# A transformer block's second LayerNorm: which engine centres it and which computes its variance

## The chip, the cores and the metric

The kernel runs on one core of a Trainium2 chip, in fp32 throughout. The metric is the device time of one execution in microseconds, lower is better; a kernel is run several times and the median counts.

## The reference

The input `x` is (16, 128, 96, 96): 16 images, 128 channels, 9216 pixels each. Cut to what matters, the block is:

```python
x_hwc = x.transpose(0, 2, 3, 1)
xn1 = layernorm(x_hwc)                           # over the 128 channels, eps 1e-5
q, k, v = xn1 @ wq.T, xn1 @ wk.T, xn1 @ wv.T     # 8 heads of 16 channels
q, k = l2norm(q), l2norm(k)                      # over the pixels of an image
attn = softmax(q k^T / 4)                        # 16 x 16 for each head, contracted over all pixels
x = x + ((attn @ v) @ wp.T)
xn2 = layernorm(x)                               # over the 128 channels again ("LN2")
h1 = conv1x1(xn2, w_in)                          # 128 -> 512 channels
h2 = depthwise_conv3x3(h1, w_dw)                 # each channel by itself
out = x + conv1x1(gelu(h2), w_out)               # 512 -> 128
```

## The kernel before

**Tiling.** Channels lie on the 128 partitions and pixels along the free dimension. An image has 8 bands of 12 rows (1152 pixels), and a band has 3 units of 4 rows (384 pixels) and 9 tiles of 128 pixels. The 512 hidden channels are 4 chunks of 128. There are 128 bands in all.

**The norms.** Both LayerNorms work on groups of 4 tiles of 128 pixels (`pixels`, 18 groups an image, 288 for all images). TensorE brings a group to pixels on partitions (`forth`), so that channels lie along the free dimension. The variance is found, GpSimd turns it into 1/sqrt(var + eps) with one multiply-add (`variance`) and one power (`power`), ScalarE scales the tile into SBUF (`scaled`), and TensorE transposes it back (`back` in `channels`), after which ScalarE copies it to its place (`place`). In LN1 the scaled tile also goes into a Gram matrix (`gram`, line 678), from which the attention of an image is worked out without q and k ever being formed.

LN1 does not subtract the mean; its weights are centred instead. LN2 has two forms here. In two groups of three, `forth` is a transpose (line 610), VectorE computes mean and variance (`stats`, line 624), `shift` makes -mean/std on VectorE (line 641), and ScalarE applies scale and bias at once (line 668). In every third group (`squares`), `forth` is a product with the matrix I - 1/128 (line 608), which transposes and subtracts the mean together; ScalarE squares each tile and sums the squares in its accumulator (`squared`, line 617), and scales without a bias (line 664). The first groups of image 0 (`early`) use other banks, and VectorE scales half of each.

**The feed-forward part.** A job is one chunk of one band (`conv_job`): TensorE forms the hidden rows (`hidden`, line 896), ScalarE copies them out of PSUM (`kept`, line 901), and the 3x3 depthwise convolution is made of nine shifted products. VectorE does 5 or 6 of them (`tap`, line 914, one pass over 128 x 1152 each), ScalarE does 2 or 3 (`product`, line 909), and DMAs that add into SBUF put the latter together (`add_products`, line 918, issued on GpSimd's queue). GELU follows on ScalarE (line 922).

The last chunk (`PE_CHUNK`) is done otherwise in some bands (`by_matmuls`): TensorE multiplies the normed rows by nine composed 128 x 128 matrices into one PSUM bank, 9 products for each of the 3 units (line 964), and ScalarE applies GELU from PSUM (line 970). Such a band needs no job for that chunk. `by_pe` chooses the bands: every second one, and six of the last eight. Four products with w_out (line 987) and one addition on VectorE (line 994) end a unit, and SyncE's queue stores a band.

An fp32 product is two passes on TensorE in the profile (so 27 products of a convolved band are 54 rows), a transpose is one.

**The order.** Nothing is scheduled at run time. `Plan` collects all operations with an engine, an estimated duration, a place and the buffers they need, plays them through a priority queue, and the order in which they start there is the order in which they are issued. Each engine then works through its own queue strictly in that order and waits at semaphores. `AT` and `STEP` hold the offset of each kind of operation from its band. Buffers that matter: 2 PSUM banks for `forth` (`tr`), 1 for `back`, 4 for the hidden rows, convolutions and outputs together (`h`), 10 SBUF buffers for the results of the convolution (`h3`) and 5 for ScalarE's products (`pr`).

Of the kernel before, what the change touches and what calls it, by code (L numbers as in the profile page):

```python
# [9 lines left out]
F32 = mybir.dt.float32  # L10
AF = mybir.ActivationFunctionType
# [6 lines left out]
UR = 4  # L18
BR = 12
PE_CHUNK = 3  # L20
PE_BANDS = (0,)
PE_OF = 2
PE_LAST = (0, 1, 2, 4, 5, 7)
TINY = 1e-20
UNIT_MIN = 1e-18
# [3 lines left out]
QT, QB = 4, 1  # L29
H_BANKS = 4  # L30
X1_BUFS, XB_BUFS, PR_BUFS, H3_BUFS, ZT_BUFS = 2, 6, 5, 10, 3
SQ_OF, SQUARED = 3, (0,)
IN_TURN = ("tr", "h3", "pr", "xb", "x1")
AT = dict(
    weights=165.45, zeros=121.05, load_a=-89.25, forth_a=1.7, stats_a=-26.4, variance_a=10.25, power_a=75.3,
    scaled_a=-4.95, gram=3.45, back_a=-204.3, place_a=63.85, attention=-94.6, mix=-102.65, residual=301.65,
    mixed=-85.2, add_x=89.65, forth_b=3.2, stats_b=-63.7, variance_b=165, power_b=182.8, shift_b=-95.45,
    scaled_b=139.5, back_b=-179.7, place_b=-67.95, squared=39.9, halo=146.15, hidden=5.1, kept=-94.75,
    products=-76.65, add_last=123.75, tap=7.3, add_first=-186.6, gelu=51.85, conv=4.7, conv_gelu=7, out=8.4,
    add=-77.85, store=98.15,  # L40
)
STEP = dict(scaled=0.3, hidden=0.1, products=0.5, tap=0.166, conv=1.6, conv_tap=0.03, out=0.8, out_part=0.05)
SLACK = 300
# [164 lines left out]
def tile_restormer_block(  # L208
# [142 lines left out]
    def at(kind, place):  # L351
        return place + AT[kind]
# [34 lines left out]
    def act(ns, p, f, r, w):  # L387
        op("ACT", ns, p, f, r, w, ns + 150 + SLACK, ns + 150)
# [158 lines left out]
    def norm(i, second, place_of):  # L547
# [5 lines left out]
        def xtok(u):  # L553
            return (x_key(i, u // UPB, second), (i, u // UPB), u % UPB)
# [34 lines left out]
        def pixels(s, m):  # L589

            d = {}
            qs = range(m * QB, (m + 1) * QB)
            early = i == 0 and (not second or m < EARLY)
            key_ = "h" if early else "tr"
            by_dve = QT // 2 if early else 0
            squares = second and not early and m % SQ_OF in SQUARED

            def forth(q):
                if early:
                    d["pT", q] = bank((name, q)).rearrange("p (t c) -> p t c", c=P)  # L600
                else:
                    d["pT", q] = p_tr.tile([P, QT, P], F32, tag="tr", name=f"pT_{name}_{q}")
                for k in range(QT):
                    b, j = divmod(q * QT + k, TPB)
                    xt = (xbs if x_key(i, b, second) == "xb" else x1s)[i, b]
                    xk = xt[:, j * P : (j + 1) * P]
                    if squares:
                        nc.tensor.matmul(d["pT", q][:, k, :], lhsT=xk, rhs=centring, start=True, stop=True)  # L608
                    else:
                        nc.tensor.transpose(d["pT", q][:, k, :], xk, ident)  # L610

            def squared(q):
                if q == qs[0]:
                    d["st"] = small.tile([P, QB * QT], F32, tag="ss", name=f"ss_{name}_{m}")
                for k in range(QT):
                    t = (q - qs[0]) * QT + k
                    nc.scalar.activation(junk, d["pT", q][:, k, :], AF.Square, accum_out=d["st"][:, t : t + 1])

            def stats(j):

                if j == 0:
                    d["st"] = small.tile([P, QB * QT // 2, 6], F32, tag="st", name=f"st_{name}_{m}")
                h, k = divmod(2 * j, QT)
                nc.vector.bn_stats(  # L624
                    d["st"][:, j, :], d["pT", qs[h]][:, k : k + 2, :].rearrange("p t c -> p c t")
                )

            def variance():
                if not squares:
                    d["mv"] = d["st"].rearrange("p j (t v) -> p (j t) v", v=3)  # L630
                of = d["st"] if squares else d["mv"][:, :, 2]
                ve = d["ve"] = small.tile([P, QB * QT], F32, tag="ve", name=f"ve_{name}_{m}")
                nc.gpsimd.tensor_scalar(ve, of, 1.0 / C, EPS, ALU.mult, ALU.add)  # L633

            def power():
                rstd = d["rstd"] = small.tile([P, QB * QT], F32, tag="rstd", name=f"rstd_{name}_{m}")
                nc.gpsimd.tensor_tensor(rstd, d["ve"], mhalf, ALU.pow)  # L637

            def shift():
                nb = d["nb"] = small.tile([P, QB * QT], F32, tag="nb", name=f"nb_{name}_{m}")  # L640
                nc.vector.scalar_tensor_tensor(nb, d["mv"][:, :, 1], -1.0, d["rstd"], ALU.mult, ALU.mult)  # L641

            def zT(q):
                zTs[q] = zT_bufs[plan.slot["zT", (name, q)]]
                return zTs[q]

            def also_scaled(q):
                for k in range(by_dve):
                    t = (q - qs[0]) * QT + k
                    if not second:  # L650
                        nc.vector.tensor_scalar(
                            zT(q)[:, k, :P], d["pT", q][:, k, :], d["rstd"][:, t : t + 1], None, ALU.mult
                        )
                        continue
                    nc.vector.tensor_scalar(
                        zT(q)[:, k, :P], d["pT", q][:, k, :], d["mv"][:, t, 1:2], d["rstd"][:, t : t + 1],
                        ALU.subtract, ALU.mult,
                    )

            def scaled(q):  # L660
                for k in range(by_dve, QT):
                    t = (q - qs[0]) * QT + k
                    if not second or squares:
                        nc.scalar.activation(  # L664
                            zT(q)[:, k, :P], d["pT", q][:, k, :], AF.Copy, scale=d["rstd"][:, t : t + 1]
                        )
                        continue
                    nc.scalar.activation(  # L668
                        zT(q)[:, k, :P], d["pT", q][:, k, :], AF.Identity,
                        bias=d["nb"][:, t : t + 1], scale=d["rstd"][:, t : t + 1],  # L670
                    )

            def gram(q):
                if q == 0:
                    grams[i] = p_g.tile([P, 4 * P], F32, tag="g", name=f"g_{i}")
                for k in range(QT):
                    zt = zTs[q][:, k, :]
                    nc.tensor.matmul(  # L678
                        grams[i][:, : P + 1], lhsT=zt[:, :P], rhs=zt,
                        start=(q == 0 and k == 0), stop=(q == NU * TPU // QT - 1 and k == QT - 1),  # L680
                    )

            trs, bt = [(key_, (name, q)) for q in qs], ("batch", (name, m))
            for q, tr in zip(qs, trs):
                units = {t // TPU: None for t in range(q * QT, (q + 1) * QT)}
                pe((220 if squares else 110) * QT, at("forth" + ab, s), lambda q=q: forth(q), [xtok(u) for u in units], [tr])
            for q, tr in zip(qs, trs) if squares else ():
                act(QT * 295, at("squared", s), lambda q=q: squared(q), [tr], [bt])
            for j in range(0 if squares else QB * QT // 2):
                dve(341, at("stats" + ab, s), lambda j=j: stats(j), [trs[2 * j // QT]], [bt])  # L690
            op("POOL", T_VARIANCE, at("variance" + ab, s), variance, [], [bt], T_VARIANCE + 33 + SLACK)
            op("POOL", T_POWER, at("power" + ab, s), power, [], [bt], T_POWER + 33 + SLACK)
            if second and not squares:
                dve(80, at("shift" + ab, s), shift, [], [bt])
            for h, (q, tr) in enumerate(zip(qs, trs)):
                zt, sh = ("zT", (name, q)), s + STEP["scaled"] * h
                if by_dve:
                    dve(by_dve * 240, at("scaled" + ab, sh), lambda q=q: also_scaled(q), [tr, bt], [(*zt, 0)])
                act((QT - by_dve) * (343 if second and not squares else 250), at("scaled" + ab, sh), lambda q=q: scaled(q), [tr, bt], [(*zt, 1)])
                if not second:  # L700
                    pe(QT * 220, at("gram", sh), lambda q=q: gram(q), [(*zt, 0), (*zt, 1), ("w", "ones")], [("g", i)])

# [369 lines left out]
```

## Time and profile before

| | |
|---|---|
| median of 3 runs | 4224.22 us (4222.87 to 4229.13) |
| the profiled execution: its own time | 4229.13 us |
| its span in the trace | 4227.4 us |
| granted TensorE clock, mean | 0.998 |
| busy in the span: TensorE matmuls, weight loads | 4190.0 us, 2725.4 us |
| busy: VectorE, ScalarE, GpSimd | 4036.8, 3780.7, 2473.4 us |
| DMA, q0 (the adding DMAs), share of 16 engines | 83.6% |
| DMA, q1 (loads and stores), share of 16 engines | 9.9% |

The profile is of one execution. Busy time is the union of the instructions' spans on an engine. Instructions of ScalarE, VectorE and TensorE overlap their successors by some 0.1 to 0.2 us, so the mean duration of one instruction is longer than what one more of its kind costs. In the timeline the cost is read as the distance from one start to the next where no wait is noted. A row of the timeline gives start, duration, engine, line, operation, result and operands, the count of merged instructions, and in brackets the idle time before it with its releaser.

### The profile page before, as it was taken

Reading aid. Unit: us, or ns where it says so; the run is one execution under the profiler, and the core shown is the slowest. Engines: PE = TensorE matmul, PEld = TensorE weight load, DVE = VectorE, ACT = ScalarE, POOL = GpSimd, SP = SyncE. Lnnn points to the kernel's source line nnn. Section 1 sums busy time; section 2 is a strip of 40 time slices with the busy share of each in tenths; the row PEclk is TensorE's granted clock in tenths of the full one; section 3 lists DMA queues with packets and bytes.
Section 4 is the critical chain, followed back from the end, with each engine's and each line's share of the span. In section 5 each row is a group of like instructions: output and inputs, shape, how many; then the busy total and the mean of one; then the engine's idle time right before and its main releaser. Section 6 shows DMA issues by size and latency. Waiting matters only on the chain. (4 is left out here: it accounts for less than half of the span.)

```text
span 4227.4 us, 53445 instructions
## 1 busy us (share of the span) xinstructions
PE 4190.0 (99%) x17833; PEld 2725.4 (64%) x17833; DVE 4036.8 (95%) x4394; ACT 3780.7 (89%) x7722; POOL 2473.4 (59%) x2373
## 2 busy tenths in 40 slices
PE   8999999999999999999999999999999999999999
PEld 6666666666666666666666666666666666666555
DVE  6999999999999999999999999999999999999998
ACT  4999999999999999999999999999989989998885
POOL 3657567565665746656475565656656566565442
PEclk9999999999999999999999999999999999999999
DMA  2999999999999999999999999999989999998997
GB/s 85 190 198 205 204 201 209 199 206 192 212 197 201 204 193 206 197 200 209 189 204 200 204 201 193 210 198 205 202 182 205 201 199 197 200 206 179 198 191 157
DMA packets 203940, 827.71 MB, mean 196 GB/s; under 512 B 23568, under 2 KB 24976, under 8 KB 203664
## 3 DMA queue, kind: packets, MB, share of 16 engines
q0 software_dynamic: 164160, 672.47, 83.6%
q1 hardware_dynamic: 37152, 151.01, 9.9%
q8 instruction: 141, 2.31, 0.2%
q10 hardware_dynamic: 2352, 0.81, 0.1%
q14 instruction: 135, 1.11, 0.1%
HBM read 148.26 MB, written 75.50 MB: 53 GB/s over the span
## 5 line engine op out<-in xcount | busy, mean ns | idle before, releaser
L914 DVE SCALAR_TENSOR_TENSOR h<-h,ratio,h 128x1152 f32<-128x1152 f32 x2104 | 2924.9, 1407 | 14.8
L909 ACT ACTIVATE pr<-h,ratio 128x1152 f32<-128x1152 f32 x1018 | 1291.1, 1286 | 41.2 <-DMA h<-pr 18.8
L964 PE MATMUL h<-xn,comp 128*128 128x384 f32 x3564 | 1250.1, 485 | 0.2 <-ACT h L901 0.2
L987 PE MATMUL h<-h,woutT 128*128 128x384 f32 x3072 | 1133.6, 488 | 2.2 <-ACT h L901 2.2
L896 PE MATMUL h<-xn,winT 128*128 128x384 f32 (+1 forms) x2676 | 1054.9, 500 | 2.4 <-ACT h L901 1.7
L964 PEld LDWEIGHTS h<-xn,comp 128*128 128x128 f32 x3564 | 648.6, 189 | 394.3 <-issue 5.6
L918 POOL DMA_DIRECT2D pr<-pr x573 | 542.2, 961 | 582.6 <-ACT pr L909 388.9
L901 ACT COPY h<-h 128x384 f32<-128x384 f32 (+1 forms) x1338 | 659.9, 516 | 159.8 <-PE h L896 152.1
L987 PEld LDWEIGHTS h<-h,woutT 128*128 128x128 f32 x3072 | 557.2, 190 | 335.4 <-issue 19.5
L914 DVE SCALAR_TENSOR_TENSOR h<-h,ratio 128x1152 f32<-128x1152 f32 x446 | 627.4, 1409 | 66.2 <-ACT h L901 54.7
L896 PEld LDWEIGHTS h<-xn,winT 128*128 128x128 f32 x2676 | 476.8, 190 | 282.0 <-issue 47.9
L918 POOL DMA_DIRECT2D h<-pr x445 | 429.3, 966 | 383.6 <-DVE h L914 94.0
L922 ACT ACTIVATE h<-h 128x1152 f32<-128x1152 f32 x448 | 531.5, 1187 | 24.7 <-DMA h<-pr 21.5
L637 POOL TENSOR_TENSOR rstd_b<-ve_b,mhalf 128x4 f32<-128x4 f32 x288 | 502.1, 1744 | 14.4
L637 POOL TENSOR_TENSOR rstd_a<-ve_a,mhalf 128x4 f32<-128x4 f32 x288 | 497.2, 1727 | 12.7 <-POOL ve_a L633 0.2
L633 POOL TENSOR_SCALAR ve_a<-st_a 128x4 f32<-128x4 f32 x288 | 296.0, 1028 | 287.7 <-DVE st_a L624 282.7
L664 ACT ACTIVATE zT<-pT_a,rstd_a 128x128 f32<-128x128 f32 x1080 | 315.1, 404 | 16.1 <-POOL rstd_a L637 15.9
L678 PEld LDWEIGHTS g<-zT 128*128 128x128 f32 x2304 | 294.1, 192 | 41.0 <-issue 2.6
L633 POOL TENSOR_SCALAR ve_b<-st_b 128x4 f32<-128x4 f32 x194 | 217.6, 1122 | 172.4 <-DVE st_b L624 165.8
L678 PE MATMUL g<-zT 128*128 128x129 f32 x2304 | 306.9, 276 | 0.0
L668 ACT ACTIVATE zT<-pT_b,nb_b,rstd_b 128x128 f32<-128x128 f32 x756 | 287.0, 477 | 12.1 <-DVE nb_b L641 11.8
L563 PE MATMUL h<-xn,mwT 128*128 128x384 f32 x768 | 282.0, 488 | 1.9 <-ACT zT L668 0.6
(178 smaller groups left out, 3950.5 us busy)
## 6 DMA issues: line engine op xcount, KB each, us to landing
pr<-pr POOLq DMA_DIRECT2D x573, 576.0 KB, 7.3
h<-pr POOLq DMA_DIRECT2D x445, 576.0 KB, 7.4
x<-in_x_dram SPq DMA_DIRECT2D x128, 576.0 KB, 6.8
out_dram<-x SPq DMA_DIRECT2D x127, 576.0 KB, 6.7
x<-in_x_dram POOLq DMA_DIRECT2D x122, 576.0 KB, 7.3
out_dram<-x SPq DMA_DIRECT2D x3, 192.0 KB, 1.9
weights<-in_L_conv_w_in_dram ACTq DMA_DIRECT2D x1, 256.0 KB, 11.1
weights<-in_L_conv_w_out_dram ACTq DMA_DIRECT2D x1, 256.0 KB, 12.0
```

Source lines behind the costliest of these rows:

```text
L633: nc.gpsimd.tensor_scalar(ve, of, 1.0 / C, EPS, ALU.mult, ALU.add)
L637: nc.gpsimd.tensor_tensor(rstd, d["ve"], mhalf, ALU.pow)
L664: nc.scalar.activation(zT(q)[:, k, :P], d["pT", q][:, k, :], AF.Copy, scale=d["rstd"][:, t : t + 1])
L678: nc.tensor.matmul(grams[i][:, : P + 1], lhsT=zt[:, :P], rhs=zt, start=(q == 0 and k == 0), stop=(q == NU * TPU // QT - 1 and k == QT - 1),)
L896: nc.tensor.matmul(rows(ph), lhsT=winT[:, n, :], rhs=window(xn, r0 + r, e - r, 1), start=True, stop=True)
L901: nc.scalar.copy(window(h1_, r, e - r, 1), rows(d.pop(("ph", r))))
L909: nc.scalar.activation(to, shifted(t), AF.Copy, scale=ratio[:, n, t : t + 1])
L914: nc.vector.scalar_tensor_tensor(h3, shifted(t), ratio[:, n, t : t + 1], onto, ALU.mult, ALU.add)
L918: nc.gpsimd.dma_start(out=to, in_=d["pr", t], accum_op=ALU.add)
L922: nc.scalar.activation(h3, h3, AF.Gelu)
L964: nc.tensor.matmul(d["pc"], lhsT=comp[:, t, :], rhs=window(xn, r0 + dy, UR, dx), start=(t == 0), stop=(t == 8),)
L987: nc.tensor.matmul(rows(d["po"]), lhsT=woutT[:, n, :], rhs=h3s[g, n][:, s * UR : (s + 1) * UR, :], start=(k == 0), stop=(k == NCH - 1),)
```

## The change

All LN2 groups, those of the start included, now take the form with the centring product and ScalarE's squares; the form with transpose, VectorE statistics, `shift` and bias is gone. The chunk that TensorE convolves is taken in 3 bands of 7 in place of 1 of 2, and in the same six of the last eight. All offsets in `AT` are new, and so the order of all queues. The core of the diff:

```diff
-PE_BANDS = (0,)
-PE_OF = 2
+PE_BANDS = (0, 2, 4)
+PE_OF = 7
...
-SQ_OF, SQUARED = 3, (0,)
+ACT_STATS = (False, True)
...
-    weights=165.45, zeros=121.05, load_a=-89.25, forth_a=1.7, stats_a=-26.4, variance_a=10.25, power_a=75.3,
...
+    weights=280.5, zeros=97.3, load_a=-104.05, forth_a=0.1, stats_a=-61.75, variance_a=134.45, power_a=-94.85,
...
-            squares = second and not early and m % SQ_OF in SQUARED
+            squares = ACT_STATS[second]
...
-                    if squares:
-                        nc.tensor.matmul(d["pT", q][:, k, :], lhsT=xk, rhs=centring, start=True, stop=True)
+                    if second or squares:
+                        nc.tensor.matmul(
+                            d["pT", q][:, k, :], lhsT=xt[:, j * P : (j + 1) * P], rhs=centring, start=True, stop=True
+                        )
                     else:
-                        nc.tensor.transpose(d["pT", q][:, k, :], xk, ident)
+                        nc.tensor.transpose(d["pT", q][:, k, :], xt[:, j * P : (j + 1) * P], ident)
...
-            def shift():
-                nb = d["nb"] = small.tile([P, QB * QT], F32, tag="nb", name=f"nb_{name}_{m}")
-                nc.vector.scalar_tensor_tensor(nb, d["mv"][:, :, 1], -1.0, d["rstd"], ALU.mult, ALU.mult)
...
                 for k in range(by_dve, QT):
                     t = (q - qs[0]) * QT + k
-                    if not second or squares:
-                        nc.scalar.activation(
-                            zT(q)[:, k, :P], d["pT", q][:, k, :], AF.Copy, scale=d["rstd"][:, t : t + 1]
-                        )
-                        continue
                     nc.scalar.activation(
-                        zT(q)[:, k, :P], d["pT", q][:, k, :], AF.Identity,
-                        bias=d["nb"][:, t : t + 1], scale=d["rstd"][:, t : t + 1],
+                        zT(q)[:, k, :P], d["pT", q][:, k, :], AF.Copy, scale=d["rstd"][:, t : t + 1]
                     )
...
-            if second and not squares:
-                dve(80, at("shift" + ab, s), shift, [], [bt])
```

By the built programs the change is, in instructions: squares on ScalarE 376 to 1152 tiles; LN2 products with the centring matrix 376 to 1152 and LN2 transposes 776 to none; VectorE statistics of LN2 388 to none and `shift` 194 to none; convolved bands 66 to 57, so products of line 964 from 1782 to 1539; jobs of that chunk 62 to 71; taps on VectorE 2550 to 2604; ScalarE's products 1018 to 1036 and with them the adding DMAs.

More of the change, by code (lines that the diff above doesn't have):

```diff
@@ L31 @@
 X1_BUFS, XB_BUFS, PR_BUFS, H3_BUFS, ZT_BUFS = 2, 6, 5, 10, 3
-SQ_OF, SQUARED = 3, (0,)
+ACT_STATS = (False, True)
 IN_TURN = ("tr", "h3", "pr", "xb", "x1")
 AT = dict(
-    weights=165.45, zeros=121.05, load_a=-89.25, forth_a=1.7, stats_a=-26.4, variance_a=10.25, power_a=75.3,
[L36 to L40, printed above, removed]
+    weights=280.5, zeros=97.3, load_a=-104.05, forth_a=0.1, stats_a=-61.75, variance_a=134.45, power_a=-94.85,
+    scaled_a=-25.95, gram=-72.35, back_a=-145.1, place_a=40.1, attention=-101.25, mix=-124.65, residual=-29.95,
+    mixed=-182.6, add_x=36.1, forth_b=0.15, stats_b=-184.75, variance_b=-169.9, power_b=-123, scaled_b=234.65,
+    back_b=-57.35, place_b=165.45, halo=235.55, hidden=3.95, kept=-96.65, products=47.7, add_last=-139.2,
+    tap=0.3, add_first=64.75, gelu=172.5, conv=4.1, conv_gelu=-0.05, out=8.2, add=-30.9, store=115.05,
 )
@@ L605, in forth @@
                     xt = (xbs if x_key(i, b, second) == "xb" else x1s)[i, b]
-                    xk = xt[:, j * P : (j + 1) * P]
-                    if squares:
-                        nc.tensor.matmul(d["pT", q][:, k, :], lhsT=xk, rhs=centring, start=True, stop=True)
+                    if second or squares:
+                        nc.tensor.matmul(
+                            d["pT", q][:, k, :], lhsT=xt[:, j * P : (j + 1) * P], rhs=centring, start=True, stop=True
+                        )
                     else:
-                        nc.tensor.transpose(d["pT", q][:, k, :], xk, ident)
+                        nc.tensor.transpose(d["pT", q][:, k, :], xt[:, j * P : (j + 1) * P], ident)
             def squared(q):
@@ L628, in variance @@
             def variance():
-                if not squares:
-                    d["mv"] = d["st"].rearrange("p j (t v) -> p (j t) v", v=3)
-                of = d["st"] if squares else d["mv"][:, :, 2]
+                of = d["st"] if squares else d["st"].rearrange("p j (t v) -> p (j t) v", v=3)[:, :, 2]
                 ve = d["ve"] = small.tile([P, QB * QT], F32, tag="ve", name=f"ve_{name}_{m}")
@@ L649, in also_scaled @@
                     t = (q - qs[0]) * QT + k
-                    if not second:
-                        nc.vector.tensor_scalar(
-                            zT(q)[:, k, :P], d["pT", q][:, k, :], d["rstd"][:, t : t + 1], None, ALU.mult
-                        )
-                        continue
                     nc.vector.tensor_scalar(
-                        zT(q)[:, k, :P], d["pT", q][:, k, :], d["mv"][:, t, 1:2], d["rstd"][:, t : t + 1],
-                        ALU.subtract, ALU.mult,
+                        zT(q)[:, k, :P], d["pT", q][:, k, :], d["rstd"][:, t : t + 1], None, ALU.mult
                     )
@@ L662, in scaled @@
                     t = (q - qs[0]) * QT + k
-                    if not second or squares:
-                        nc.scalar.activation(
-                            zT(q)[:, k, :P], d["pT", q][:, k, :], AF.Copy, scale=d["rstd"][:, t : t + 1]
-                        )
-                        continue
                     nc.scalar.activation(
-                        zT(q)[:, k, :P], d["pT", q][:, k, :], AF.Identity,
-                        bias=d["nb"][:, t : t + 1], scale=d["rstd"][:, t : t + 1],
+                        zT(q)[:, k, :P], d["pT", q][:, k, :], AF.Copy, scale=d["rstd"][:, t : t + 1]
                     )
@@ L685, in pixels @@
                 units = {t // TPU: None for t in range(q * QT, (q + 1) * QT)}
-                pe((220 if squares else 110) * QT, at("forth" + ab, s), lambda q=q: forth(q), [xtok(u) for u in units], [tr])
+                pe((220 if second or squares else 110) * QT, at("forth" + ab, s), lambda q=q: forth(q), [xtok(u) for u in units], [tr])
             for q, tr in zip(qs, trs) if squares else ():
-                act(QT * 295, at("squared", s), lambda q=q: squared(q), [tr], [bt])
+                act(QT * 295, at("stats" + ab, s), lambda q=q: squared(q), [tr], [bt])
             for j in range(0 if squares else QB * QT // 2):
@@ L698, in pixels @@
                     dve(by_dve * 240, at("scaled" + ab, sh), lambda q=q: also_scaled(q), [tr, bt], [(*zt, 0)])
-                act((QT - by_dve) * (343 if second and not squares else 250), at("scaled" + ab, sh), lambda q=q: scaled(q), [tr, bt], [(*zt, 1)])
+                act((QT - by_dve) * 250, at("scaled" + ab, sh), lambda q=q: scaled(q), [tr, bt], [(*zt, 1)])
                 if not second:
```

## The prediction

> **What bounds the kernel now.** I read the busy shares first, then the starts in TensorE's timeline, then the chain and the waits.
>
> ```profile
> PE 4190.0 (99%) x17833; PEld 2725.4 (64%) x17833; DVE 4036.8 (95%) x4394; ACT 3780.7 (89%) x7722; POOL 2473.4 (59%) x2373
> q0 software_dynamic: 164160, 672.47, 83.6%
> ```
>
> Three engines and the DMAs look nearly full, so busy shares alone decide nothing. TensorE's starts do:
>
> ```profile
> 2008.98 1.05 PE L608 MATMUL pT_b<-centring,x 128*128 128x128 f32 x8
> 2009.86 0.81 PE L964 MATMUL h<-xn,comp 128*128 128x384 f32 x2
> ...
> 2017.88 0.49 PE L711 MATMUL pB_a<-ident,zT 128*128 128x128 f32 x3
> 2018.21 0.60 PE L610 MATMUL pT_a<-ident,x 128*128 128x128 f32 x4
> 2018.65 0.81 PE L964 MATMUL h<-xn,comp 128*128 128x384 f32 x2
> 2019.29 1.05 PE L678 MATMUL g<-zT 128*128 128x129 f32 x8
> ...
> 4208.37 15.49 PE h L987 x48
> ```
>
> The first rows are the timeline, the last is the chain's end, where the kernel finishes on 48 passes at 0.323 us. No row has idle time in brackets: each starts when the one before has streamed. Four transposes take 2018.65 - 2018.21 = 0.44 us, 0.109 each; eight centring passes take 0.88 us, 0.111 each; a pass over 384 columns takes 0.322. The lower quartile of the distances between starts, over the whole trace, gives the same paces, 0.402 for 480 columns and 0.109 for 129. So TensorE's work in passes is: line 964, 3564 x 0.322 = 1148 us; line 987, 3072 x 0.322 = 989; line 896, 2236 x 0.323 + 440 x 0.402 = 899; line 563, 768 x 0.322 = 247; Gram and back transposes, 4608 x 0.109 = 502; forward transposes, 1928 x 0.109 = 210; centring, 752 x 0.111 = 83; attention and weights about 57. Together 4135 us of a span of 4227.4. The other 92 are 6 before the first pass, 4 after the last, and 82 of waits and jitter, 27 of them in the first 200 us. From then on TensorE loses 55 us in 4000. It is the bound, and the clock can't move much: the granted mean is 0.998.
>
> **The other engines**, by the same paces: VectorE 3972 us (2550 taps at 1.325, 964 statistics at 0.341, 384 additions at 0.467, small ones), ScalarE 3653. ScalarE's rows:
>
> ```profile
> 2006.08 1.19 ACT L664 ACTIVATE zT<-pT_a,rstd_a 128x128 f32<-128x128 f32 x4
> 2007.09 3.62 ACT L909 ACTIVATE pr<-h,ratio 128x1152 f32<-128x1152 f32 x3
> 2010.53 0.65 ACT L715 ACTIVATE xn<-pB_b,b 128x384 f32<-128x384 f32 x1
> ...
> 2054.24 0.28 ACT L617 ACTIVATE junk<-pT_b 128x128 f32<-128x128 f32 x1
> 2054.41 0.20 ACT L617 ACTIVATION_READ_ACCUMULATOR junk<-pT_b 128x1 f32 x1
> 2054.63 1.28 ACT L922 ACT_TABLE_LOAD   x1
> 2055.92 1.16 ACT L922 ACTIVATE h<-h 128x1152 f32<-128x1152 f32 x1
> 2056.99 1.49 ACT L668 ACTIVATE zT<-pT_b,nb_b,rstd_b 128x128 f32<-128x128 f32 x4
> 2058.36 0.27 ACT L860 COPY y<-g 128x128 f32<-128x128 f32 x1
> ```
>
> A square with its accumulator read costs 2054.63 - 2054.24 = 0.39 us (0.394 over the trace), a scaling with bias (2058.36 - 2056.99)/4 = 0.342, without it 1.01/4 = 0.252 (0.249 over the trace), one of the big products 3.44/3 = 1.147, a GELU of a band 1.054.
>
> **The change on TensorE**, which is on the path all along. Nine bands lose 54 passes each: 9 x 54 x 0.322 = -156.5 us. Their jobs add two products of 480 and one of 384 columns: 9 x (4 x 0.402 + 2 x 0.322) = +20.3. 776 tiles turn from a transpose into two centring passes: 776 x (0.222 - 0.109) = +87.7. The sum is -48.5: TensorE's work falls to 4087 us.
>
> *A rule against it.* The row says that a centring product costs 0.222 us where a transpose costs 0.109. The Trainium skill (Perfetto Trace Analysis, section Transposes) says that a logical transpose should be issued as a transpose and not as an ordinary product. By the rule alone the change loses the 87.7 us; the trace agrees on the price, but not on the verdict, since convolutions worth more leave the same engine.
>
> *A rule on the bound.* Between starts nothing waits, in rows with 0.19 us of weight load under 0.32 us of matmul. The same page (section Identifying the Most-Contended Engine) would have TensorE judged by weight-load busy time, not matmul busy time. By it (64%) there is a third of the engine free, ScalarE at over 95% would bind after the change, and the 48.5 us would be worth nothing: about 4224 us. I go by the starts.
>
> **On VectorE:** 9 jobs of 6 taps, 54 x 1.325 = +71.6; 388 statistics x 0.341 = -132.3; 194 shifts x 0.073 = -14.2; ten half-scalings lose their subtraction, -0.7. Together -75.6: 3897 us, all under TensorE's cover.
>
> **On ScalarE:** 776 squares x 0.394 = +305.7; 766 scalings x (0.342 - 0.249) = -71.2; in nine bands three copies (2 x 0.439 + 0.359), two products (2 x 1.147) and one GELU of a band for three of a unit (1.054 - 3 x 0.370), 9 x 3.48 = +31.3. Together +266: 3919 us. That lies beside TensorE's 4087 with 168 us to spare, much as VectorE's 3972 lay beside 4135 with 163. Without that cover it is the first rival.
>
> **On GpSimd and the DMAs:** its variance and power counts stay. 18 more adding DMAs cost 18 x 0.96 = 17 us of issue on an engine at 59%. One holds the 16 DMA engines 0.836 x 4227/1140 = 3.10 us (1140 with the 122 that add x), so q0 rises by 56 to 3590 us, 85.7% of the new span. ScalarE's own waits on DMAs are 59 us now (21.5 + 18.8 + 18.6); scaled by the idle share of q0, 16.4% to 14.3%, they become 68, which ScalarE's spare time hides. Loads and stores keep their number on SyncE's queue.
>
> **The wait that moves.** In 194 groups GpSimd's variance now waits for ScalarE's squares instead of VectorE's statistics. Behind it in GpSimd's queue stand adding DMAs, and for those wait GELU and then line 987. The rows for the two forms are these:
>
> ```profile
> POOL ve_b L633 <- DVE st_b L624: 165.8, 90, 6.4
> POOL ve_b L633 <- ACT junk L617: 129.6, 65, 7.0
> ACT h L901 <- PE h L896: 152.1, 266, 3.4
> DVE h L914 <- ACT h L901: 54.7, 42, 3.6
> PE pB_b L711 <- ACT zT L664: 1.9, 2, 1.6
> ```
>
> Per group that is 0.85 us now (165.8/194) against 1.38 (129.6/94): 288 groups would make GpSimd wait about 397 us where it waits 295, and it has over 1700 us without busy time. TensorE itself lost next to nothing to such chains (last row).
>
> **What the new order costs** the trace can't show. TensorE was fed beside one engine with 163 us to spare; it will be fed beside two with 168 and 190. Its gaps of over 0.2 us after the start sum to 26 us. From below, half of these could go (-13); from above stand the rivals' prices. I take +13, half of the 26 again for the second tight engine, as the nearest row is VectorE's: tight, and nearly harmless. Span: 4087 + 92 + 13 = 4192. The profiled span lies 3.2 us above the median of the runs (4227.4 against 4224.2), so I say 4189. What is late next would be ScalarE.
>
> **Rival 1, ScalarE becomes the bound (slower).** Its queue is strict, and today it idles 574 us beside its 3653. Part of that is being early, part is bursts that a fuller queue doesn't remove: waits on TensorE (lines 901, 970, 717, 715, 572: 152.1 + 38.3 + 41.8 + 36.5 + 10.6 = 279), on DMAs 59, on GpSimd and VectorE about 40, together 378. If all stay, the span is 3919 + 378 = 4297, 4294 by the median. It decides from 317 us of remaining waits on (4236 - 3919, 0.2% over the median before). For it: the largest of these waits, line 901, comes 266 times and isn't one of slack only. Against it: VectorE ran with 255 us between pace and span, and ScalarE would have 273 at my forecast.
>
> **Rival 2, lumpier bands.** Every seven bands now hold two in a row without TensorE's convolution. Such a band asks VectorE for 23 taps x 1.325 + 3.5 = 34.0 us (3.5: the rest of its 3897, over 128 bands) and TensorE for (4087 - 57 x 17.4 - 71 x 2.25)/128 + 2.25 = 25.2. Before, no two such bands came together. If none of the second one's difference is bridged, TensorE waits 8.8 us in 17 places: 150 us, 4339. With half of it bridged it is 75 us in place of my 13, 4251. It costs the whole gain at 48 us. Ten `h3` buffers, two and a half bands, speak against it.
>
> **How the numbers follow.** My forecast has 0.55, with its own range 4163 (gaps halve) to 4215; rival 1 has 0.22, from 4233 to 4294; rival 2 has 0.18, from 4205 to 4339; a start or an end that the new order makes worse has 0.05, around 4220. The range 4163 to 4262 leaves out a little below (0.03), half of rival 1 and a quarter of rival 2, some 0.18 in all. A measurement of this kernel can tell 0.2%, 8.4 us, from no change. Faster: 0.53 of the forecast and 0.03 of rival 2, 0.56. Within 0.2%: 0.10, from the last case and rival 2. Slower: rival 1 and most of rival 2, 0.34.
>
> **What would show it.** Right: TensorE's starts still close up, with paces 0.322 and 0.111 and no bracketed idle time; distances beyond the pace near 95 us in all; ScalarE at about 95 to 97% busy, VectorE near 94%. Rival 1 shows as waits of TensorE's and VectorE's rows on ScalarE (zT, h of line 901's successor) of a hundred us and more; rival 2 as waits that return every seven bands, some 230 us apart. If the accumulator read costs more in a full queue than 0.394 us a square, ScalarE's term is wrong; if TensorE's paces stretch, all of it is.

## The result and the profile after

The changed kernel takes 4255.39 us (median of 4 runs, 4252.32 to 4258.21) against 4225.37 of the kernel before: ratio 1.0070, 95% interval 1.0053 to 1.0088. It is slower by 30 us; 36 less were forecast. The page of its profiled execution (span 4256.5 us), the lines that answer to those of before:

```profile
PE 4178.0 (98%) x18177; PEld 2737.5 (64%) x18177; DVE 3971.5 (93%) x3866; ACT 3952.2 (93%) x9301; POOL 2434.6 (57%) x2391
...
q0 software_dynamic: 166752, 683.09, 82.8%
```

By the same paces as in the prediction, TensorE's work is now 4087 us, ScalarE's 3919 and VectorE's 3912 (forecast 4087, 3919 and 3897). The counting was right; what lies around TensorE's work was not. I call that the *waits* of a kernel from here on: its median less the sum of TensorE's paces, good to some 3 us. Before they were 90, after they are 168.

The waits of the weight loads show the same. Each row gives what waited, for whom, the sum in us, the count and the longest; after, and then before:

```profile
PEld h L876 <- ACT h L881: 26.1, 44, 1.6
...
PEld pB_b L691 <- ACT zT L651: 19.0, 56, 3.0
```

```profile
PEld h L896 <- ACT h L901: 7.6, 18, 1.3
...
PEld pB_b L711 <- ACT zT L664: 5.1, 10, 2.2
```

All such waits on ScalarE together grew from 81 to 212. So far this reads as rival 1. But the waits come in a rhythm. The next rows are the changed kernel's windows, cut at the last output product (line 967) of each band of one period of seven: start and end, length, busy us and count of each engine, granted clock, DMA share and GB/s. The bands, in order: not convolved on TensorE, convolved, not, convolved, not, **not**, convolved.

```profile
2590.30:2617.30 27.00, 26.96 (x101) 16.38 (x100) 25.28 (x21) 26.48 (x62) 11.02 (x12) 1.00 0.84 175
2617.30:2647.50 30.20, 30.20 (x112) 18.68 (x111) 29.92 (x27) 25.73 (x58) 14.80 (x16) 1.00 1.01 209
2647.50:2679.10 31.60, 31.60 (x146) 21.30 (x145) 28.93 (x28) 30.94 (x73) 20.02 (x19) 1.00 1.00 210
2679.10:2697.70 18.60, 18.60 (x74) 11.51 (x73) 18.60 (x19) 18.18 (x40) 11.28 (x12) 1.00 1.00 223
2697.70:2738.70 41.00, 40.94 (x190) 27.52 (x189) 41.00 (x39) 39.87 (x100) 28.62 (x26) 1.00 0.98 205
2738.70:2783.00 44.30, 38.44 (x173) 26.91 (x172) 39.26 (x38) 38.30 (x88) 33.06 (x25) 0.92 0.85 179
2783.00:2824.00 41.00, 39.80 (x192) 27.34 (x191) 33.88 (x35) 36.67 (x90) 24.95 (x25) 1.00 0.95 195
```

The steady bands leave TensorE no hole; the second of the double bands has 44.30 - 38.44 = 5.9 us without a matmul, the one after it 1.2. Summed over bands 4 to 119, the distances of TensorE's starts beyond the pace are 29.3 us in the stretches that end with the first band of a double, 39.9 in those of the second, and 7.9 to 11.8 in each of the other five. That is rival 2's mark.

One such hole, in the timeline of the changed kernel, by start:

```profile
2745.61 0.41 DVE L624 BATCH_NORM_STATS2 st_a<-pT_a 128x6 f32<-128x256 f32 x1
...
2747.27 1.40 DVE L894 SCALAR_TENSOR_TENSOR h<-h,ratio 128x1152 f32<-128x1152 f32 x1
2747.74 10.30 POOL L631 TENSOR_SCALAR ve_a<-st_a 128x4 f32<-128x4 f32 x1
2748.60 5.39 DVE L894 SCALAR_TENSOR_TENSOR h<-h,ratio,h 128x1152 f32<-128x1152 f32 x4
2753.92 1.40 DVE L894 SCALAR_TENSOR_TENSOR h<-h,ratio 128x1152 f32<-128x1152 f32 x1
2755.25 2.73 DVE L894 SCALAR_TENSOR_TENSOR h<-h,ratio,h 128x1152 f32<-128x1152 f32 x2
...
2758.12 1.03 POOL L635 TENSOR_TENSOR rstd_a<-ve_a,mhalf 128x4 f32<-128x4 f32 x1
2759.19 1.14 ACT L651 ACTIVATE zT<-pT_a,rstd_a 128x128 f32<-128x128 f32 x4 [4.64 <-POOL rstd_a L635]
2759.61 2.09 PE L660 MATMUL g<-zT 128*128 128x129 f32 x8 [2.94 <-ACT zT L651]
```

The last statistics before it end at 2746.02. GpSimd's multiply-add on 128 x 4 elements, which takes 0.18 us at its shortest, starts at 2747.74 and ends at 2758.04, when VectorE's eight taps in a row end. Then power, scaling and TensorE follow at once. ScalarE, named as TensorE's releaser, had itself been waiting. This was in no rival; it is theory F below, where it is also counted how much of the 168 us comes this way.

### The profile page after: what moved, and what is told of

It is laid out like the page before. It is cut to its first block, busy times and chain, and to the rows that moved or that the text cites. A ratio compares the mean times of both kernels' runs of the same rounds, so it can differ in the third digit from the quotient of the medians.

```text
span 4256.5 us, 55284 instructions
## 1 busy us (share of the span) xinstructions
PE 4178.0 (98%) x18177; PEld 2737.5 (64%) x18177; DVE 3971.5 (93%) x3866; ACT 3952.2 (93%) x9301; POOL 2434.6 (57%) x2391
## 3 DMA queue, kind: packets, MB, share of 16 engines
q0 software_dynamic: 166752, 683.09, 82.8%
## 4 chain that ended last, share of the span: by engine, by line
PE 37%; ACT 11%; DVE 4%; DMA 2%; issue 2%; POOL 1%; POOLq 0%; ACTq 0%; DVEq 0%
PE h L967 9%; PE h L944 9%; PE h L876 8%; DVE h L894 4%; ACT pr L889 3%; PE pT_b L606 2%; PE h L562 2%; PE g L660 2%; ACT zT L651 2%; ACT h L902 1%; ACT h L881 1%; ACT junk L617 1%; DMA h<-pr 1%; PE pB_b L691 1%; PE pB_a L691 1%
## 5 line engine op out<-in xcount | busy, mean ns | idle before, releaser
L894 DVE SCALAR_TENSOR_TENSOR h<-h,ratio,h 128x1152 f32<-128x1152 f32 x2149 | 2971.2, 1409 | 17.4
L889 ACT ACTIVATE pr<-h,ratio 128x1152 f32<-128x1152 f32 x1036 | 1344.9, 1305 | 33.9 <-DMA h<-pr 19.3
L944 PE MATMUL h<-xn,comp 128*128 128x384 f32 x3078 | 1109.8, 486 | 0.8 <-ACT h L881 0.7
L944 PEld LDWEIGHTS h<-xn,comp 128*128 128x128 f32 x3078 | 560.4, 189 | 344.2 <-ACT h L881 5.3
L898 POOL DMA_DIRECT2D h<-pr x454 | 471.6, 1039 | 237.8 <-DVE h L894 45.9
L902 ACT ACTIVATE h<-h 128x1152 f32<-128x1152 f32 (+1 forms) x457 | 549.7, 1206 | 10.3 <-DMA h<-pr 10.0
L635 POOL TENSOR_TENSOR rstd_b<-ve_b,mhalf 128x4 f32<-128x4 f32 x288 | 481.0, 1670 | 13.6
L631 POOL TENSOR_SCALAR ve_b<-ss_b 128x4 f32<-128x4 f32 x288 | 224.3, 779 | 441.6 <-ACT junk L617 441.3
L617 ACT ACTIVATE junk<-pT_b 128x128 f32<-128x128 f32 x1132 | 330.1, 292 | 89.2 <-PE pT_b L606 60.7
L651 ACT ACTIVATE zT<-pT_b,rstd_b 128x128 f32<-128x128 f32 x1132 | 335.3, 420 | 11.7 <-POOL rstd_b L635 11.5
L651 ACT ACTIVATE zT<-pT_a,rstd_a 128x128 f32<-128x128 f32 x1080 | 319.0, 417 | 14.8 <-POOL rstd_a L635 14.5
```

The lines of the kernel that those rows point to most:

```text
L651: nc.scalar.activation(zT(q)[:, k, :P], d["pT", q][:, k, :], AF.Copy, scale=d["rstd"][:, t : t + 1])
L889: nc.scalar.activation(to, shifted(t), AF.Copy, scale=ratio[:, n, t : t + 1])
L894: nc.vector.scalar_tensor_tensor(h3, shifted(t), ratio[:, n, t : t + 1], onto, ALU.mult, ALU.add)
L898: nc.gpsimd.dma_start(out=to, in_=d["pr", t], accum_op=ALU.add)
L902: nc.scalar.activation(h3, h3, AF.Gelu)
L944: nc.tensor.matmul(d["pc"], lhsT=comp[:, t, :], rhs=window(xn, r0 + dy, UR, dx), start=(t == 0), stop=(t == 8),)
```

## The experiments

The theories as they stood: A, ScalarE is too full (rival 1); B, double bands (rival 2); C, the order was planned with squares at 295 ns where they cost 394; D, both ScalarE and VectorE hold a part; E, neither. F came last: unbroken runs of taps keep GpSimd out, and TensorE waits for 1/sqrt. Where a kernel leaves instructions out, the queues keep their order, so that only the load changes.

**One square in four left out.** TensorE's work 4086, waits 149.

```diff
-                for k in range(QT):
+                for k in range(QT - 1):
```

> The changed kernel in the same order of every queue, but ScalarE leaves out the square of the fourth tile of each LN2 group (a constant stands in for its sum): 288 squares less, 288 x 0.394 = 113 us of ScalarE's 3919, and nothing else. TensorE's work stays at 4087 us; the changed kernel lost 169 us around it (span 4256). Theory A, ScalarE is too full and TensorE waits for it: most of the 77 us of added waits go, about 4185 to 4205. Theory B, the two bands in a row without convolution are the cause and VectorE is late there: little changes, 4240 to 4255. Theory C, the order was planned with squares that are too cheap (295 ns in the plan, 394 in the trace; three squares cost 1.18 us, what the plan has for four): 4185 to 4205 as well, told apart from A by the run with the corrected plan.

4235.24 us (4229.09 to 4244.13), ratio 1.0028 (1.0019 to 1.0037). 20 us came back, between the forecasts of A and B: neither alone.

**71 taps left out, in the bands that aren't convolved.**

```diff
+            if n == PE_CHUNK and t == left[-1] and not last:
+                return
```

> The changed kernel in the same order, but VectorE leaves out the last tap of each job of the last chunk: 71 taps less, 71 x 1.325 = 94 us, all of them in bands that TensorE doesn't convolve. Theory B (lumps, VectorE late in the double bands): VectorE's 34.0 us for such a band become 32.7, and a good part of the added waits goes, 4200 to 4225. Theory A or C: little changes, 4240 to 4255.

4244.06 us, ratio 1.0046 (1.0031 to 1.0061): 11 us.

**The same number of taps left out evenly.**

```diff
+            if n == 0 and g % 9 in (0, 2, 4, 6, 8) and t == left[-1]:
+                return
```

> The changed kernel in the same order, but VectorE leaves out the last tap of the first chunk's job in 71 bands spread evenly: the same 94 us off VectorE, not aimed at the bands without convolution. Theory B: it helps less than taking them out where the lump is, 4220 to 4240. A VectorE that is merely too full everywhere would show the same gain in both. Theory A or C: 4240 to 4255.

4242.73 us, ratio 1.0041 (1.0027 to 1.0055): 13 us, no less than where the lump is. Relief aimed at the lump bought no more than relief elsewhere.

**The plan's price corrected.**

```diff
-                act(QT * 295, at("stats" + ab, s), lambda q=q: squared(q), [tr], [bt])
+                act(QT * 394, at("stats" + ab, s), lambda q=q: squared(q), [tr], [bt])
```

> The changed kernel with one number of the plan changed: a square is planned at 394 ns, as the trace has it, in place of 295. No work is added or left out; the order of the queues moves. Theory C: the waits fall to those of the kernel before, 4190 to 4215. Theory A or B: within 20 us of the changed kernel, 4235 to 4275.

4281.84 us, ratio 1.0136 (1.0121 to 1.0151): worse than any theory had it. The offsets in `AT` fit one set of prices; with another they are just other offsets. So where a later kernel is said to have its offsets searched anew, it has the corrected price and offsets from a new random search with the plan as its measure, equally long for each.

**The same with offsets searched anew.** Same work as the changed kernel.

> The changed kernel's work to the last instruction, with a square planned at 394 ns as measured, and with all offsets searched anew for that plan (in the run with the corrected price alone the old offsets no longer fitted: 4282). Theory C (an order planned with a wrong price): 4190 to 4220. Theories A, B, D: the loads are the same, so the waits stay, 4240 to 4265.

4248.51 us, ratio 1.0048 (1.0033 to 1.0063), waits 164. Price and search together are worth 7 us. C falls.

**Three of four squares left out; 199 taps left out; both.**

```diff
-                for k in range(QT):
+                for k in range(1):
...
+            if n in (0, PE_CHUNK) and t == left[-1] and not last:
+                return
```

> The changed kernel in the same order of every queue, ScalarE leaves out three of the four squares of each LN2 group (a constant stands in for their sums): 864 x 0.394 = 340 us off ScalarE, whose 3919 us become 3579, less than the 3653 of the kernel before. TensorE's 4087 stay. Leaving out one square in four gave 20 us. Theory A (a full ScalarE is what TensorE waits for): TensorE's waits fall to those of the kernel before, about 4180 to 4195. Theory B (two bands in a row without convolution, VectorE late there): a floor of about 4220 to 4235 is left. Theory D (both engines hold a part): 4200 to 4220.

> The changed kernel in the same order, VectorE leaves out the last tap of every job of the first and the last chunk: 199 taps, 199 x 1.325 = 264 us off VectorE's 3912. Leaving out 71 gave 11 to 13 us. Theory B: 4190 to 4215. Theory A: nothing beyond the 13 us had already, 4235 to 4245. Theory D: 4215 to 4235.

> The changed kernel in the same order with both left out, 340 us of squares on ScalarE and 264 us of taps on VectorE, so that TensorE's 4087 us stand over 3579 and 3648. Theories A, B and D: TensorE has nothing to wait for but the start, 4165 to 4190. If it stays over 4200, the waits come from neither engine's load but from the order itself or the DMAs (theory E).

The busy lines of the three, in that order:

```profile
PE 4155.6 (98%) x18177; PEld 2747.0 (65%) x18177; DVE 3968.8 (94%) x3866; ACT 3694.0 (87%) x7573; POOL 2499.7 (59%) x2395
```

```profile
PE 4170.1 (98%) x18177; PEld 2734.4 (64%) x18177; DVE 3725.2 (88%) x3667; ACT 3955.7 (93%) x9301; POOL 2337.4 (55%) x2391
```

```profile
PE 4142.5 (99%) x18177; PEld 2742.9 (66%) x18177; DVE 3723.2 (89%) x3667; ACT 3696.0 (88%) x7573; POOL 2398.6 (57%) x2395
```

4227.65 us, ratio 1.0002 (0.9992 to 1.0012); 4240.98, 1.0031 (1.0019 to 1.0044); 4187.29, 0.9904 (0.9889 to 0.9919). The first lies in B's range, the second in A's, the third in that of A, B and D. Alone they give 28 and 14 us, together 68, and waits of 104. With ScalarE at 87%, looser than the 89% of before, some 143 us of waits are still there: A falls as the whole cause. A part of why the two give more together is in the traces: with the squares out ScalarE's waits for 1/sqrt from GpSimd rise to 50.7 us, with the taps out as well they are 20.3. That otherwise each relief alone leaves the other engine in the way is argued.

**The changed kernel's loads without double bands.** Every second band convolved, with one product of nine left out; 55 taps and 64 squares done twice; offsets searched anew. So TensorE keeps 4092 us, VectorE and ScalarE 3912 each.

```diff
-PE_BANDS = (0, 2, 4)
-PE_OF = 7
+PE_BANDS = (0,)
+PE_OF = 2
...
-        for t in range(9):
+        for t in (0, 1, 2, 3, 5, 6, 7, 8):
...
+        if n == 0 and g % 7 in (0, 2, 4):
+            left.append(8)
```

> The loads of the changed kernel without its lumps. LN2 as in the changed kernel, but TensorE convolves every second band, as before, and leaves out one of the nine products of each, so that its work is 4087 + 136 - 127 = 4096 us; 55 taps are done once more, spread evenly, so that VectorE keeps its 3913 (changed kernel 3912), and 64 squares are done twice (ScalarE 3913 against 3919). Offsets searched anew in the same way and for as long as in the retuned run of the changed kernel, which took 4248.5. Theory B (two bands in a row without convolution): waits fall to 90 to 105 us beside the 4096, 4185 to 4200. Theory A or D (two engines at 95% each, wherever their work lies): waits stay near 165, 4250 to 4265.

4210.86 us, ratio 0.9964 (0.9951 to 0.9977), waits 118 against the retuned kernel's 164. The kernel without double bands waits **46 us** less. It lies between B's range and that of A and D: B holds, at a third of its full price of 150. Each of the two is one order, though, and the changed kernel's work took 4248.51, 4255.39 and 4281.84 us in three. 28 us more than before stay.

**The same two with three of four squares left out.**

> The even kernel (loads of the changed kernel, no double bands; 4210.9, 114 us around TensorE's 4092) in the same order, with three of the four squares of each group left out and the doubled ones single: 928 x 0.394 = 366 us off ScalarE's 3912. If ScalarE's fullness holds what the lumps don't: waits of 85 to 95, 4175 to 4190. If VectorE's 3912 beside 4092 hold it: 4200 to 4211.

> The retuned changed kernel (4248.5, 161 us around TensorE's 4085) in the same order, with three of the four squares of each group left out: 340 us off ScalarE. If lumps and a full ScalarE add up, about 25 us go and 47 for the lumps stay: 4218 to 4228. If lumps only hurt where ScalarE is full too, the waits fall to those of the even kernel without squares: 4180 to 4200.

4198.79 us, ratio 0.9938 (0.9923 to 0.9953), and 4228.04 us (4214.77 to 4236.50), ratio 1.0004 (0.9991 to 1.0018). The first falls between its two forecasts, the second on the edge of the one by which lumps and squares add up. A table of the waits:

| | all squares | one in four |
|---|---|---|
| double bands (retuned) | 164 | 143 |
| none (even) | 118 | 106 |

Lumps cost 37 to 46, squares on ScalarE 12 to 21. The corner with neither still loses 16 more than the kernel before, which these four kernels don't explain.

**The two parts alone**, offsets searched anew: LN2 with bands as before, and bands with LN2 as before.

```diff
-PE_BANDS = (0, 2, 4)
-PE_OF = 7
+PE_BANDS = (0,)
+PE_OF = 2
```

> The first part of the change alone: all LN2 groups by centring product and squares, bands as before (every second one), offsets searched anew. TensorE 4135 + 88 = 4223 us, ScalarE 3888, VectorE 3841, 92% and 91% of TensorE's. Theories B and D: waits of 80 to 100, 4300 to 4320. Theory A: ScalarE at 3888 idles less beside it than in the kernel before, up to 4340.

4342.44 us, ratio 1.0277 (1.0261 to 1.0292): TensorE 4221, waits 122. That is **32 more than before**, above what B and D had and 2 us above A's upper edge, without any double band.

```diff
-PE_BANDS = (0,)
-PE_OF = 2
+PE_BANDS = (0, 2, 4)
+PE_OF = 7
```

> The second part alone: LN2 as before, TensorE convolves 3 bands of 7, offsets searched anew. TensorE 4135 - 136 = 3999 us, VectorE 3972 + 72 = 4044, ScalarE 3684. VectorE becomes the bound. With about 90 us around it the span would be 4135; theory B, TensorE waits in the 17 double bands and VectorE in the others: 4180 to 4230; theory A: 4130 to 4160, since ScalarE is loose.

4235.66 us (4231.12 to 4245.46), ratio 1.0026 (1.0016 to 1.0035): 191 us beside VectorE's 4045, with ScalarE loose. It missed B's range from above, and A's by 76.

32 of the LN2 part and 46 of the double bands make 78, the growth from 90 to 168. It is a sum over kernels with different orders, so no proof, and the changed kernel's trace divides the 78 otherwise, as shown below. What makes the 32?

**VectorE's run of taps broken up.** The LN2 part took 388 statistics and 194 shifts out of VectorE's queue, and these had stood between the taps. Counting taps that follow one another with nothing between, the kernel before has 37 runs of 7 or more, the LN2 part alone 76, the changed kernel 103. Two kernels add useless VectorE work to the LN2 part alone:

```diff
             nc.vector.scalar_tensor_tensor(h3, shifted(t), ratio[:, n, t : t + 1], onto, ALU.mult, ALU.add)
+            if t in (left[1], left[3]):
+                nc.vector.scalar_tensor_tensor(gap_, mhalf, -1.0, mhalf, ALU.mult, ALU.mult)
```

> The LN2 part alone (4342.4), same order, plus a VectorE operation on 128 x 4 elements after the second and the fourth tap of every job, 892 in all, 892 x 0.073 = 65 us more on VectorE (3847 to 3912 beside TensorE's 4221). Theory F (unbroken runs of taps keep GpSimd out, and TensorE waits for 1/sqrt): GpSimd gets in at the breaks, 4320 to 4335. Otherwise VectorE is only fuller: 4342 to 4355.

4304.41 us (4302.24 to 4307.86), ratio 1.0187 (1.0170 to 1.0204). 892 additional instructions make the kernel **38 us faster**; the waits are 83, less than the 90 before the change. The groups of lines, of the LN2 part alone and then of the kernel with the breaks (count, busy, mean ns, idle before and releaser):

```profile
L651 ACT ACTIVATE zT<-pT_b,rstd_b 128x128 f32<-128x128 f32 x1132 | 328.8, 396 | 55.5 <-POOL rstd_b L635 54.9
L631 POOL TENSOR_SCALAR ve_b<-ss_b 128x4 f32<-128x4 f32 x288 | 263.3, 914 | 311.9 <-ACT junk L617 310.6 <-DMA pr<-pr 0.5
```

```profile
L652 ACT ACTIVATE zT<-pT_b,rstd_b 128x128 f32<-128x128 f32 x1132 | 328.6, 396 | 24.9 <-POOL rstd_b L636 24.4 <-PE g L661 0.2
L632 POOL TENSOR_SCALAR ve_b<-ss_b 128x4 f32<-128x4 f32 x288 | 211.9, 736 | 304.1 <-ACT junk L618 301.4 <-DVE gap L897 2.1 <-DMA pr<-pr 0.2
```

ScalarE's wait for 1/sqrt falls from 54.9 to 24.4 us. Of GpSimd's 1152 variance and power operations, 15 took over 3 us and the longest 10.7; with the breaks none does. The kernel before has 8, the longest 6.8.

> The same with one longer operation in place of two short ones: a statistics instruction over 128 x 128 after the third tap of every job, 446 in all, about 0.2 us each, 90 us on VectorE. Theory F: 4320 to 4335, at least as good as the short ones, since a statistics instruction reads one operand only. Otherwise 4342 to 4360.

With one statistics instruction in each of 446 jobs: 4311.79 us (4307.48 to 4315.57), ratio 1.0206 (1.0190 to 1.0221), 31 us faster. F holds for the LN2 part alone, beyond what either run expected. Its five longest holds, of 10.70, 9.60, 8.45, 8.15 and 6.28 us, each end in a hole of TensorE of 2 to 7 us, and they make nearly all of this row of TensorE's waits, which stands at 0.6 with the breaks and stood at 1.9 in the kernel before:

```profile
PE pB_b L691 <- ACT zT L651: 26.0, 6, 7.1
```

**What of this the changed kernel has.** ScalarE's waits for 1/sqrt, in the changed kernel and then in the kernel before:

```profile
ACT zT L651 <- POOL rstd_a L635: 14.5, 13, 4.6
ACT zT L651 <- POOL rstd_b L635: 11.5, 14, 3.0
```

```profile
ACT zT L664 <- POOL rstd_a L637: 16.2, 23, 2.2
ACT zT L664 <- POOL rstd_b L637: 10.0, 9, 3.2
```

That is 26 us in both. Of GpSimd's 1152 operations 5 take over 3 us in the changed kernel, fewer than the 8 before, and after the first 200 us the hole shown above is the only one of over 2 us that starts from one of them. So F, which explains most of the LN2 part's 32 us, explains next to nothing of the changed kernel's 78.

Where the 78 lie is told by the distances of TensorE's starts beyond the pace. Here they are summed over bands 4 to 119 (us, one execution each), apart for the 32 bands that are part of a double in the changed kernel and for the other 84:

| | the 32 | the 84 |
|---|---|---|
| before | 14.8 | 35.1 |
| changed | 69.2 | 51.4 |
| changed, three of four squares left out | 68.7 | 29.2 |
| changed, 199 taps left out | 60.3 | 47.0 |
| changed, both left out | 36.2 | 24.4 |
| the same loads without double bands (even, an order of its own) | 20.4 | 43.0 |

The double bands have 54 us of the growth, close to the 46 above; the other bands have 16, and 8 more lie in the first four bands. In the other bands it is ScalarE's squares: without them the distances fall below those of before. In the double bands neither relief alone does much, and both together take off half.

**A middle way.** Every second LN2 group squared, 5 bands of 11 (then 6 of 13), and as a control the kernel before with its offsets searched anew; all with the corrected price.

```diff
-SQ_OF, SQUARED = 3, (0,)
+SQ_OF, SQUARED = 2, (0,)
...
-PE_BANDS = (0,)
-PE_OF = 2
+PE_BANDS = (0, 2, 4, 6, 8)
+PE_OF = 11
```

> A middle way, with everything computed: every second LN2 group by centring product and squares, TensorE convolves 5 bands of 11, offsets searched anew. TensorE 4135 + 188 x 0.113 - 5 x 15.1 = 4081 us, VectorE 3976, ScalarE 3727, a double band only every 11 bands. If a loose ScalarE is what keeps TensorE fed (theories A and D), waits of 90 to 120 us: 4170 to 4200. If every double band costs 3 to 4 us (B), 11 of them add 35 to 45: 4200 to 4215.

> The mixed kernel with 6 bands of 13 in place of 5 of 11, all computed, offsets searched anew: 62 convolved bands in place of 61, so TensorE 4094 us, VectorE 3984, a double band every 13 in place of every 11. If the loads limit (TensorE's 4079 in the mixed kernel): 4200 to 4212. If the doubles do: 4185 to 4195.

> The kernel before, all its work unchanged, a square planned at 394 ns, offsets searched anew in the same way and for as long as in the mixed kernel. If the search is the mixed kernel's gain: 4195 to 4210. If the mix is: 4220 to 4235, the search alone being worth no more than the 7 us it was worth in the changed kernel.

```profile
PE 4141.0 (99%) x17781; PEld 2700.7 (64%) x17781; DVE 4016.2 (96%) x4283; ACT 3812.4 (91%) x8113; POOL 2482.1 (59%) x2383
```

The mixed kernel (its busy line above) takes **4193.59 us**, ratio 0.9923 (0.9906 to 0.9939), faster than the kernel before and the changed one, and in the range of A and D; TensorE's work is 4079, the waits 115. The second mix takes 4195.11, 0.9930 (0.9915 to 0.9945): 15 us more on TensorE and 14 less of waits, as fewer double bands would have it. The control takes 4221.40, 0.9987 (0.9978 to 0.9997): this search is worth 4 us, the mix the rest. Breaks between the taps were not tried in the mixed kernel; its ScalarE waits 24.9 us for 1/sqrt, no more than in the kernel before.

## Why the prediction was wrong

**TensorE's sum** held: -48.5 us forecast, 4135 to 4087 measured. Reading the bound off the starts and not off busy shares or weight loads was right. The Trainium skill (Perfetto Trace Analysis, section Identifying the Most-Contended Engine) names weight-load busy time as one of its two measures of TensorE's headroom. By it TensorE, at 64% before and after, would have had room; the kernel that took load off both other engines and none off TensorE stopped at 104 us above TensorE's paces.

**ScalarE's sum** held (3919), the accumulator read included; VectorE's missed by 15 us, its taps being paced at 1.327 and not 1.320 at the lower quartile. GpSimd's wait for the squares, forecast at 397 us, was 441. ScalarE's waits on DMAs, forecast at 68, were 43 (19.3 + 13.8 + 10.0); the adding DMAs' queue, forecast to rise to 3590 us of the 16 engines, took 3524 (82.8% of 4256.5).

**The step that failed is "What the new order costs".** I took +13 us; it was +78, from 90 us of waits to 168. The reason given, that VectorE was "tight, and nearly harmless" before, carried a row of one tight engine and an even rhythm over to two tight engines and an uneven one. What the runs showed in its place:

- *Double bands*, 54 of the 78 by the trace, 46 by the kernel without them, where the forecast had none. Rival 2 had the place and the rhythm, and its full price was some three times too high; with half of the difference bridged it said 4251, and that 4255 was measured is partly luck, since 24 of the 78 lie elsewhere. (Its 4339 adds the 150 to a forecast that holds the 13; in place of them it is 4326.)
- *ScalarE's squares in the other bands*, 16 us: **rival 1** as a part. Over all bands leaving out squares gives 12 to 21 us in retuned orders, 28 with the changed order.
- *The first four bands*, 8 us, whose cause stays open.

That the two reliefs give 68 together and 28 and 14 alone was in neither the forecast nor a rival. That 4255 lies inside the range of 4163 to 4262 owes to the rivals' part of that range; the forecast itself was a faster kernel.

*VectorE's removed statistics*, which I counted as -75.6 us of work "all under TensorE's cover", were not free in the LN2 part alone: the longer runs of taps held GpSimd up, and through it TensorE, as the breaks show. I named what is queued behind the waiting variance, but not what holds GpSimd itself. In the changed kernel, which has still more of these runs (103 against 76), that made one hole of 3 us. Why the holds hit TensorE in one order and not in another stays open.

Breaks were tried neither in the changed kernel nor in the kernel before. Open stays also what of bands_alone's 191 us around VectorE each cause has: of TensorE's distances there 105 us lie in the 32 double bands and 70 in the other 84. And what a fuller search would give each kernel isn't known.

## What to carry to other kernels

When the engine that bounds a kernel loses work, sum the paces as here, but price the feeding by what the queues look like, not by shares: where the load of neighbouring stages differs, and which short instructions break up the long ones. An instruction that costs an engine 0.07 us may be worth more than its price if a neighbour is held up without the gap it makes. A mechanism that is seen once in a timeline is counted over the whole trace, in the kernel before as well, ahead of being given the difference. A relief that shows little alone should be tried together with the next tightest engine before its cause is dropped.

## What the runs showed of the hardware

A GpSimd operation of 0.18 us was held for 10.30 us while VectorE ran eight 128 x 1152 taps one after the other. The Trainium skill (SBUF — State Buffer, section Terms) says that VectorE and GpSimd share a pair of ports which is locked for a whole instruction, the loser being blocked. The trace agrees for most operations: of the changed kernel's 576 multiply-adds on 128 x 4 elements 534 took at most 1.5 us, where a tap takes 1.40, and some 290 ended together with a tap that another tap followed at once. So GpSimd is mostly let in at the next boundary between two taps. It isn't always: the hold above lasted over seven boundaries. With a 128 x 4 operation put in after the second and the fourth tap of every job the longest went from 10.7 to 2.9 us, though that operation reads SBUF too. What decides whether a boundary lets GpSimd in, no run shows.

After a hole of 2.94 us TensorE ran at half speed for 3.4 us: the eight passes at 2759.61 above take 1.88 us to the next start, 0.235 each where the pace is 0.109, and the window's granted clock is 0.92. Holes of 2.6, 2.6 and 1.9 us did the same, and so did shorter ones in a row (0.30, 0.45 and 0.85 us within 3 us). The length alone doesn't decide it: holes of 2.62, 2.06 and 1.99 us in the first 160 us of the same trace were followed by full speed. At half speed, 3.4 us lose up to 1.7 us of passes beside the hole, by estimate.
